# Pair 0 of the first pass: which PSUM bank each of its output blocks is accumulated in

## The chip, the cores and the metric

The kernel runs on one core of a Trainium2 chip. The metric is the device time of that core in microseconds (us). The time before is the median of three runs. One further execution was recorded by the hardware profiler, and every line and duration below comes from it.

The engines are named as in the profile: PE is the matrix engine (TensorE), PEld its weight loads, DVE the vector engine, ACT the scalar engine, POOL the GpSimd engine, SP the engine that issues most of the DMAs. Each takes its own instructions in order and waits for the others by semaphores. PE writes its results to PSUM, and DVE and ACT read them from there.

## The reference, cut to what matters

The input `x` is 128 graphs of 64 nodes with 768 features, and `adj` holds their adjacency matrices. Two layers follow each other. The change is in the first:

```
h   = max(layernorm(x), 0)
ctx = (adj @ (h @ Wadj.T + badj)) / deg + (adj.T @ (h @ Wrev.T + brev)) / rdeg + h @ Wself.T + bself
rel = sum over neighbours of E[adj] @ Wr.T + br * deg  + the same for adj.T with E, Wrr, brr
x   = x + ctx + rel
```

The entries of `adj` are 0 and 1, and the kernel treats them as ids of relations: it counts for each node how many neighbours carry each id and multiplies the counts by a table. The second layer is attention over the graphs with a gate. It is the second pass of the kernel.

## The kernel before, in words

**Tiling.** The 8192 nodes are 64 tiles of 128 rows (two graphs each), and two tiles make a pair. Pass 1 runs over the 32 pairs. The left operand of a pair is cut in six blocks `a00` to `a12`: the first digit is the tile in the pair, the second a third of the 768 inputs. The weights are cut in nine blocks `b00` to `b22` (third of the inputs, third of the outputs). A block product is six fp32 matmuls of 128x128 by 128x256, since a block holds three matrices (`Wadj`, `Wrev`, `Wself`) and two slices of 128 inputs. Each of the six output blocks of a pair (tile, third of the outputs) is then added to `x`.

Pairs 1 to 31 use a scheme with 15 products of sums of blocks (`PRODUCTS`). Pair 0 uses the plain 18 products (`PLAIN`, L73), since the sums of weights (`g10`, `w`, `u`, ...) are only being formed while it runs. Its order is: output block 00, 10, 02, 12, 01, 11, and 18 matmuls for each.

**Banks.** `product` (L741) sends its matmuls to a PSUM bank that has a letter. `new` (L716) makes the tile behind it. Letters a and b each have a tile of their own (`pwa`, `pwb`). Letters c and d are the two halves of one tile, `pwcd`, each half a bank:

```
if not CD:
    CD.append(psw.tile([P, 2, 512], F32, name="pwcd"))
bank[b] = CD[0][:, "cd".index(b)]
```

When an output block is complete, `counts` (L724) adds two bf16 matmuls of relation counts to it, and `add` (L733) has DVE add the bank to `x` (L737). The counts of blocks 00 and 10 are not ready in time in pair 0. They get two steps of their own at the end, `rest_of` (L764), each with a bank, two matmuls (L729) and a DVE add.

**Order.** The order on PE, DVE, ACT and POOL is the order in which the program is written. `main` (L711) gives a list of steps, one matmul each: 0 to 17 are block 00, 18 to 35 block 10, 36 to 53 block 02, 54 to 71 block 12, 72 to 89 block 01, 90 to 107 block 11, and then the two of `rest_of`. `merged` (L248) puts side work between them. For pair 0 that is the list `first` (L884). Of it the following matters here:

- sums of weights on DVE (`weights_sums`) at steps 19, 30, 36, 38, 60, 66 and 76
- `prep_c(1)` at step 40, `count(1, 0)` at 44 and `count(1, 1)` at 52, all DVE work that counts pair 1's ids. `add` of block 02 is at step 53, behind all of these in DVE's order
- `digits(1)` at step 58: four small DVE operations and two POOL copies (`c`, L644)
- `operand` at 54, 64 and 80: pair 1's left operand, by PE (L673) into tiles `pb`, two of which exist, and out of them by ACT (L683)
- `form` at 73 and 91: sums of operand blocks on DVE
- `count_t` at 84 and 92: PE transposes (L652) of the POOL copies

Pair 1 follows at once. Its products begin with banks b, a and d.

Of the kernel before, what the change touches and what calls it, by code (L numbers as in the profile page):

```python
# [69 lines left out]
)  # L70


PLAIN = tuple((f"a{k}{j}", f"b{j}{q}", "abcdab"[2 * i + k], j == 0, f"{k}{q}" if j == 2 else None,  # L73
               "+", i > 0) for i, q in enumerate((0, 2, 1)) for k in range(2) for j in range(3))


# [73 lines left out]
def kernel(  # L150
# [97 lines left out]
    def merged(main, side):  # L248

        side = sorted(side, key=lambda e: e[0])  # L250
        i = 0
        for n, step in enumerate(main):
            while i < len(side) and side[i][0] <= n:
                side[i][1]()
                i += 1
            step()
        for _, step in side[i:]:
            step()
# [135 lines left out]
    with ExitStack() as px:  # L394
# [316 lines left out]
        def main(p):  # L711

            bank = {}
            steps = []

            def new(b):  # L716
                if b in "ab":
                    bank[b] = psw.tile([P, 512], F32, name=f"pw{b}")
                    return
# [4 lines that stand above are left out]
            def counts(b, c, first=False):  # L724
                k, q = int(c[0]), int(c[1])
                if first:
                    new(b)
                for i, (a, e) in enumerate(PARTS):
                    nc.tensor.matmul(bank[b][:, :CQ], CT_T[p, k][: 3 * (e - a), i, :],  # L729
                                     tabs[i][:, q * CQ : (q + 1) * CQ],  # L730
                                     start=(first and i == 0), stop=True, skip_group_check=True)

            def add(b, c, sign="+"):  # L733
                k, q = int(c[0]), int(c[1])
                v = X[2 * p + k][:, q * CQ : (q + 1) * CQ]
                if sign == "+":
                    nc.vector.tensor_add(v, bank[b][:, :CQ], v)  # L737
                else:
                    nc.vector.tensor_sub(v, v, bank[b][:, :CQ])

            def product(an, bn, b, first, c, sign, cnt):  # L741
                def step(q, s):
                    if first and q == s == 0:
                        new(b)
                    nc.tensor.matmul(  # L745
                        bank[b][:, :CQ], OPS[p, an][:, s, q, :],
                        bw[bn][:, (s * KQ + q) * CQ : (s * KQ + q + 1) * CQ],
                        start=(first and q == s == 0), stop=(q == KQ - 1 and s == 2),
                        skip_group_check=True)
                    if q == KQ - 1 and s == 2 and c:  # L750
                        if cnt:
                            counts(b, c)
                        add(b, c, sign)
                for q in range(KQ):
                    for s in range(3):
                        steps.append(lambda q=q, s=s: step(q, s))

            later = (PRODUCTS[1], PRODUCTS[0], *PRODUCTS[2:]) if p + 1 < NP else PRODUCTS  # L760
            for x in later if p else PLAIN:
                product(*x)

            rest_of = ["12"] if p else ["00", "10"]  # L764
            for i, c in enumerate(rest_of):
                b = "dc"[i % 2]
                steps.append(lambda b=b, c=c: (counts(b, c, True), add(b, c)))
            return steps

# [195 lines left out]
        for p in range(NP):  # L965
            merged(main(p), beside(p) if p else first)
# [445 lines left out]
```

## Time and profile before

| | us |
|---|---|
| median of 3 runs | 2400.27 (2399.43 to 2400.63) |
| profiled execution, its own time | 2400.11 |
| its span | 2398.3 |
| PE busy | 2363.1 (99%) |
| DVE busy | 1954.2 (81%) |
| ACT busy | 1339.7 (56%) |
| POOL busy | 380.0 (16%) |

The chain of work that ended last lies on PE for 95% of the span. Times in the trace count from the span's start. Pair 0's products run from 15.05 us to 88.49 us, where the first matmul of pair 1 starts. An fp32 matmul has two records in the trace, so that the six of a block product appear as x12. In lines of the timeline the second number is the time from the first start to the last end of a merged group. Matmuls are pipelined: the next one starts a little before the modelled end of the last.

### The profile page before, as it was taken

The numbers are of one execution on the slowest core, as the hardware profiler recorded it, in microseconds if no ns is written. First come the engines' busy times: TensorE is split into PE (matmuls) and PEld (weight loads), VectorE is DVE, ScalarE is ACT, GpSimd is POOL, SyncE is SP. The second block draws the span as 40 slices with busy tenths as digits, with TensorE's granted clock in tenths as the row PEclk, the third lists the DMA queues.
The fourth block names the chain that finished last, engine by engine and source line by source line (L and its number), as shares of the span: only waits on it lengthen the run. The fifth ranks groups of instructions, "written<-read, shape, count | busy, mean of one in ns | idle before, by whom it ended". The sixth has DMA issues, their size and how long they took to land.

```text
span 2398.3 us, 35465 instructions
## 1 busy us (share of the span) xinstructions
PE 2363.1 (99%) x11777; PEld 1662.7 (69%) x11777; DVE 1954.2 (81%) x3611; ACT 1339.7 (56%) x4017; POOL 380.0 (16%) x983
## 2 busy tenths in 40 slices
PE   7999999999999999999999999999999999999997
PEld 5888888888888888888888884444444444444445
DVE  8677778778778787787787876888989888999999
ACT  2345455454454554544544524777777777767777
POOL 1111111111111111111111111111111111111122
PEclk9999999999999999999999999999999999999999
DMA  5143533534435335344353366665555555555545
GB/s 185 43 121 89 142 99 96 145 89 117 121 89 137 100 95 150 88 109 130 88 136 102 95 189 132 113 113 111 114 110 108 108 111 115 113 110 108 114 98 100
DMA packets 582906, 271.80 MB, mean 113 GB/s; under 512 B 424394, under 2 KB 533053, under 8 KB 582722
## 3 DMA queue, kind: packets, MB, share of 16 engines
q1 hardware_dynamic: 572850, 244.71, 40.3%
q0 software_dynamic: 9728, 24.78, 6.7%
q8 instruction: 93, 1.52, 0.3%
q14 instruction: 91, 0.75, 0.1%
q10 hardware_dynamic: 144, 0.04, 0.0%
HBM read 119.66 MB, written 124.26 MB: 102 GB/s over the span
## 4 chain that ended last, share of the span: by engine, by line
PE 95%; DVE 3%; ACT 2%; issue 0%; DMA 0%; SPq 0%; DVEq 0%; ACTq 0%
PE pwa L745 21%; PE pwb L745 17%; PE pwcd L745 14%; PE pma L1050 13%; PE pmb L1050 11%; PE pmc L1050 5%; PE pmd L1050 4%; PE pb L673 3%; PE ps L1203 2%; PE pwcd L729 1%; PE pwcd L673 1%; PE ps L1185 1%; ACT pr L1102 1%; PE ps L1154 1%; DVE weights L344 0%
## 5 line engine op out<-in xcount | busy, mean ns | idle before, releaser
L745 PE MATMUL pwa<-weights,op 128*128 128x256 f32 x2304 | 539.5, 381 | 0.3 <-DVE x L737 0.3
L745 PEld LDWEIGHTS pwa<-weights,op 128*128 128x128 f32 x2304 | 422.2, 190 | 53.5 <-issue 0.9
L745 PE MATMUL pwb<-weights,op 128*128 128x256 f32 x1932 | 454.2, 381 | 0.0
L745 PEld LDWEIGHTS pwb<-weights,op 128*128 128x128 f32 x1932 | 359.5, 190 | 53.0
L745 PE MATMUL pwcd<-weights,op 128*128 128x256 f32 x1560 | 360.1, 381 | 12.7 <-DVE x L737 12.7
L344 DVE TENSOR_TENSOR op<-op 128x768 f32<-128x768 f32 x310 | 291.8, 950 | 95.6 <-ACT op L683 91.7
L745 PEld LDWEIGHTS pwcd<-weights,op 128*128 128x128 f32 x1560 | 297.6, 191 | 53.9 <-DVE x L737 12.9
L1050 PE MATMUL pma<-weights,op_f 128*128 128x512 f32 x620 | 310.3, 597 | 2.6 <-ACT hh L783 2.2
L683 ACT COPY op<-pb 128x512 f32<-128x512 f32 (+1 forms) x132 | 70.8, 618 | 335.1 <-PE pb L673 335.1
L1102 ACT ACTIVATE pr<-pr 128x128 f32<-128x128 f32 x768 | 225.3, 296 | 25.1 <-DVE pr L1092 25.0
L1050 PEld LDWEIGHTS pma<-weights,op_f 128*128 128x128 f32 x620 | 112.2, 190 | 140.4 <-issue 104.6
L1050 PE MATMUL pmb<-weights,op_f 128*128 128x512 f32 x372 | 193.1, 601 | 0.4 <-DVE hz L1077 0.4
L321 POOL TENSOR_SCALAR rn<-su 128x1 f32<-128x1 f32 x124 | 27.7, 224 | 918.5 <-ACT hf L316 532.1
L531 ACT ACTIVATE hp<-x,rn 128x768 f32<-128x768 f32 x60 | 107.8, 1796 | 108.6 <-POOL rn L323 108.6
L315 ACT ACTIVATE hf<-x 128x768 f32<-128x768 f32 x64 | 53.8, 841 | 164.5 <-DVE x L781 150.2
L1102 ACT ACTIVATION_READ_ACCUMULATOR pr<-pr 128x1 f32 x768 | 144.4, 188 | 0.0
L1175 ACT ACTIVATE pb<-al,mx 128x64 f32<-128x64 f32 x384 | 128.5, 337 | 12.4 <-DVE mx L1167 11.6
L1050 PE MATMUL pmc<-weights,op_f 128*128 128x512 f32 x248 | 129.7, 604 | 0.2 <-DVE weights L1079 0.2
L1213 DVE SCALAR_TENSOR_TENSOR f<-ps,dn,bb 128x128 f32<-128x128 f32 x384 | 110.1, 344 | 21.6 <-PE ps L1203 20.3
L1050 PE MATMUL pmb<-weights,h 128*128 128x512 f32 x248 | 127.7, 596 | 0.0
L737 DVE TENSOR_TENSOR x<-pwa,x 128x256 f32<-128x256 f32 x95 | 40.1, 422 | 104.1 <-PE pwa L729 75.6
L624 DVE TENSOR_REDUCE sum<-eq 128x26 f32<-128x1664 bf16 x64 | 120.0, 1876 | 0.1
(217 smaller groups left out, 3991.1 us busy)
## 6 DMA issues: line engine op xcount, KB each, us to landing
x<-in_x_dram SPq DMA_DIRECT2D x64, 384.0 KB
h<-ht SPq DMA_DIRECT2D x64, 384.0 KB
out_dram<-x SPq DMA_DIRECT2D x64, 384.0 KB
hh<-hh SPq DMA_DIRECT2D x64, 384.0 KB
h<-h SPq DMA_DIRECT2D x256, 96.0 KB
x<-hh SPq DMA_DIRECT2D x64, 384.0 KB
out_dram<-f POOLq DMA_DIRECT2D x62, 384.0 KB, 5.0
h<-hpt SPq DMA_DIRECT2D x60, 384.0 KB
```

Of the source, the lines that this page charges most:

```text
L315: nc.scalar.activation(by, src, AF.Copy, scale=-1.0 / D, accum_out=sums[:, 0:1])
L344: return (nc.vector.tensor_add if s1 == "+" else nc.vector.tensor_sub)(to, x, y)
L531: nc.scalar.activation(hp.rearrange("p (b f i) -> p b f i", b=KB, f=NQ), X[t].rearrange("p (b i f) -> p b f i", b=KB, f=NQ), AF.Relu, scal ...
L624: nc.vector.tensor_reduce(SUM[p][:, k], EQ[p, k], AX.X, OP.add)
L673: nc.tensor.matmul(to[:, g, :, i, :], H0[2 * p + k][o, kb * P : (kb + 1) * P], rts[p % 2][o, k, :n].rearrange("p s n -> p (s n)"), start=T ...
L683: nc.scalar.copy(a[:, :n].rearrange("p s h (g n) -> p g (s h) n", g=GT), ps[:, :, c * n * KQ * N : (c + 1) * n * KQ * N].rearrange("p g (x ...
L745: nc.tensor.matmul(bank[b][:, :CQ], OPS[p, an][:, s, q, :], bw[bn][:, (s * KQ + q) * CQ : (s * KQ + q + 1) * CQ], start=(first and q == s ...
L1050: nc.tensor.matmul(bank[p, b], operand(p, an)[:, q, :], bw2[bn][:, 2 * q * CQ : 2 * (q + 1) * CQ], start=(first and q == 0), stop=(q == KQ ...
L1102: nc.scalar.activation(PR[t][:, j, h, :], PR[t][:, j, h, :], AF.Copy, accum_out=to)
L1175: nc.scalar.activation(PB[t][:, h, :], AL[t][:, h, :], AF.Exp, bias=MX[t][:, h : h + 1], accum_out=DN[t][:, h : h + 1])
L1203: nc.tensor.matmul(po[r][o, c, :], PT[t][s, c, o], (hs if r == g else HX[t])[s, 2 * c + r, :], start=True, stop=True)
L1213: nc.vector.scalar_tensor_tensor(FF[t][:, h * DO : (h + 1) * DO], PO[t][r][:, c, :], DN[t][:, h : h + 1], bb, op0=OP.mult, op1=OP.add)
```

## The change

Only letters change. Pair 0's six output blocks used banks a, b, c, d, a, b and use a, b, c, a, b, c. The two extra count steps used d and c and use a and d. Pairs 1 to 31 keep their letters, `"d" if p else ...` being what `"dc"[0]` was. No instruction is added or removed, and the order on every engine is the same.

```diff
-PLAIN = tuple((f"a{k}{j}", f"b{j}{q}", "abcdab"[2 * i + k], j == 0, f"{k}{q}" if j == 2 else None,
+PLAIN = tuple((f"a{k}{j}", f"b{j}{q}", "abcabc"[2 * i + k], j == 0, f"{k}{q}" if j == 2 else None,
                "+", i > 0) for i, q in enumerate((0, 2, 1)) for k in range(2) for j in range(3))
...
             rest_of = ["12"] if p else ["00", "10"]
             for i, c in enumerate(rest_of):
-                b = "dc"[i % 2]
+                b = "d" if p else "ad"[i]
                 steps.append(lambda b=b, c=c: (counts(b, c, True), add(b, c)))
```

| block or step | bank before | bank after |
|---|---|---|
| 00 | a | a |
| 10 | b | b |
| 02 | c | c |
| 12 | d | a |
| 01 | a | b |
| 11 | b | c |
| counts of 00 | d | a |
| counts of 10 | c | d |

## The prediction

> **What bounds the kernel now.** I read the page first, then the waits of PE, then pair 0 in the timelines of PE and DVE, then the stretches. The page says that PE is the bound, and names one product group with idle time in front of it:
>
> ```profile
> PE 2363.1 (99%) x11777; PEld 1662.7 (69%) x11777; DVE 1954.2 (81%) x3611; ACT 1339.7 (56%) x4017; POOL 380.0 (16%) x983
> ...
> L745 PE MATMUL pwcd<-weights,op 128*128 128x256 f32 x1560 | 360.1, 381 | 12.7 <-DVE x L737 12.7
> ```
>
> Of a span of 2398.3 us PE is idle some 35, and 12.7 of those stand in front of one tile. The waits of PE, longest first, show that this is a single wait, and that the same tile has a small second one:
>
> ```profile
> PE pwcd L745 <- DVE x L737: 12.7, 1, 12.7
> ...
> PE pwcd L729 <- DVE x L737: 0.6, 1, 0.6
> ```
>
> PE's timeline gives the place (start, length, group, idle before it):
>
> ```profile
> 42.75 0.39 PE L729 MATMUL pwcd<-tab,cntT 126*128 126x256 bf16 x2
> 43.07 1.57 PE L673 MATMUL pb<-r,h 64*128 64x192 f32 x16
> 57.29 6.73 PE L745 MATMUL pwcd<-weights,op 128*128 128x256 f32 x20 [12.65 <-DVE x L737]
> 63.95 1.57 PE L673 MATMUL pb<-r,h 64*128 64x192 f32 x16
> 65.45 3.72 PE L745 MATMUL pwcd<-weights,op 128*128 128x256 f32 x16
> ...
> 88.27 0.38 PE L729 MATMUL pwcd<-tab,cntT 126*128 126x256 bf16 x2 [0.62 <-DVE x L737]
> ```
>
> Block 02 (bank c) is complete at 43.1, block 12 (bank d) is next and needs nothing from it. But c and d are one tile, so its first matmul waits until DVE has read block 02. DVE's timeline shows why that is late, and what DVE has to do next:
>
> ```profile
> 55.02 1.89 DVE L624 TENSOR_REDUCE sum<-eq 128x26 f32<-128x1664 bf16 x1
> 56.82 0.41 DVE L737 TENSOR_TENSOR x<-pwcd,x 128x256 f32<-128x256 f32 x1
> ...
> 61.58 1.82 DVE L342 SCALAR_TENSOR_TENSOR weights<-weights 128x1536 f32<-128x1536 f32 x1
> 69.43 0.42 DVE L737 TENSOR_TENSOR x<-pwcd,x 128x256 f32<-128x256 f32 x1 [6.03 <-PE pwcd L729]
> 69.77 2.88 DVE L344 TENSOR_TENSOR op<-op 128x768 f32<-128x768 f32 x3
> 72.57 3.42 DVE L344 TENSOR_TENSOR weights<-weights 128x1536 f32<-128x1536 f32 x2
> 79.29 0.42 DVE L737 TENSOR_TENSOR x<-pwa,x 128x256 f32<-128x256 f32 x1 [3.31 <-PE pwa L729]
> 79.64 2.81 DVE L344 TENSOR_TENSOR op<-op 128x768 f32<-128x768 f32 x3
> 87.46 0.42 DVE L737 TENSOR_TENSOR x<-pwb,x 128x256 f32<-128x256 f32 x1 [5.01 <-PE pwb L729]
> ```
>
> DVE is busy without a break from 41.3 to 63.4 with weight sums and the counting of pair 1. The add stands behind that. Last, the stretches (us; PE, PEld, DVE, ACT, POOL busy; granted clock; DMA share; GB/s):
>
> ```profile
> 44.60:57.30 12.70, 0.05 (x3) 0.01 (x1) 12.32 (x19) 0.93 (x2) 0.00 (x0) 0.63 0.00 0
> 57.30:64.00 6.70, 6.70 (x22) 5.29 (x22) 6.00 (x8) 0.00 (x0) 3.61 (x2) 0.67 0.00 0
> 64.00:69.20 5.20, 5.20 (x35) 4.46 (x35) 0.00 (x0) 1.50 (x2) 0.00 (x0) 1.00 0.00 0
> 88.50:130.00 41.50, 41.50 (x233) 36.09 (x232) 33.17 (x54) 15.12 (x24) 4.54 (x11) 1.00 0.43 118
> ```
>
> The wait has a tail: after it PE runs at a granted clock of 0.67 until 64.0. From 88.5 on PE has no gap for 41.5 us.
>
> **What the Trainium skill says.** "TensorE: Matmul & The Clock Gate", Part 1 (The HAM clock gate): after an idle window of about 3.4 us the array's clock is gated to half, and about 3.4 us of activity release it. The trace agrees in kind: 0.67 for 6.7 us after 12.65 us idle. The same page, under engine queue depths: ACT and DVE are strict FIFO, so the add cannot pass the counting; the trace shows it directly behind. "PSUM — Partial Sum Buffer", Terms: two engines must not touch one bank at once. Here c and d are different banks, so the wait comes from the shared tile and not from that rule; the new letters put PE and DVE on different banks as well.
>
> **The change, part by part.**
>
> *Block 12 goes to bank a.* Bank a was last read by the add of block 00, at 26.99. So nothing holds its first matmul. It starts when the L673 group before it lets it: that group starts at 43.07, and the equal group at 63.95 is followed 1.50 later, so at 44.57 instead of 57.29. That is **12.72** us.
>
> *The slow clock goes too.* The 20 records after the wait take 57.29 to 63.95, 6.66 us. At full clock 12 records take 2.59 (88.49 to 91.08), so 20 take 4.32. That is **2.34** more, and PE is ahead by 15.06 at the L673 group, which now starts at 48.89. The bounds are 0, if the clock is slow there for another reason, and 2.34; I take 2.34, since the stretch before the wait (30 to 44.6) has clock 1.00.
>
> *Is anything late for a PE that is 15.06 ahead?* Operands: ACT has copied out the first `pb` tile by 45.53, before the second group of 48.89; the third group, 72.78 less 15.06 = 57.72, needs a copy that moves with PE to 49.9 to 51.4. DMA: the stretches from 44.6 to 69.2 show a share of 0.00, so the loads have landed. POOL: the two copies that the transposes need run from 58.19 to 61.80, the longer of 1.92, so the first is there by 60.11 and the second by 61.80. They follow DVE, which does not move before 63.4. PE wants them at 76.11 and 79.96 less 15.06, 61.05 and 64.90. It is close, 0.94 us, and costs nothing. Block 01 in bank b waits for the add of block 10 (40.96), block 11 in bank c for that of block 02 (56.82); PE is there at 54.17 and 64.03.
>
> *DVE becomes the late one.* It is free at 63.32 (61.58 + 1.82, less the 0.08 by which neighbours overlap). The add of block 12, which waited for PE until 69.43, finds its bank ready (PE is through at 69.40 less 15.06 = 54.34). Then, with the steps read from the rows above: add 0.34 to 63.66; three operand sums 2.80 to 66.46; two weight sums 3.34 to 69.80; add of block 01 0.34 to 70.14 (PE ready at 64.2); three operand sums 2.73 to 72.87; add of block 11 to 73.29. PE has block 11 ready at 72.36. So DVE arrives half a microsecond behind PE.
>
> *The end of pair 0.* The counts of 00 now go to bank a and start at 87.26 less 15.06 = 72.20. The counts of 10 go to d, in the tile whose half c the add of block 11 is reading: they wait for its end at 73.29 and start 0.06 later (as 88.21 to 88.27 before), at 73.35. This new wait of about 0.8 takes the place of the old 0.62. Queued behind it is all of pair 1 on PE, whose first matmul starts 0.22 later, at 73.57. Before it was 88.49: the sum is **14.92** us. DVE's adds of the two count steps end near 73.6 and 74.2; pair 1's bank a is wanted at 76.2 and bank d at 78.8, so these waits cost nothing.
>
> *Afterwards* pair 1 starts with both engines shifted by about 14.9, and its DMAs (first at 95.20) follow them. No instruction order changes. The gap-free PE carries the shift to the end. The profiled execution would take 2400.11 - 14.92 = 2385.19; the median, 0.16 above it, 2385.35.
>
> **The rivals.**
>
> *The clock's part does not come back, or comes in part.* Then only 12.65 to 13 are gained: 2387.3 to 2387.6. Against it is the 1.00 before the wait.
>
> *DVE or POOL is slower than I copied.* From 41.3 to 73.3 DVE has next to no slack, so each microsecond lost there delays pair 1 by as much; 5% of the 32 us is 1.6, giving 2387.0. A late POOL copy costs only what goes beyond 0.94. For it speaks that the POOL copies took 1.9 us here and 0.39 elsewhere, so neighbours disturb each other; against it that DVE's companions up to 63.4 are the same.
>
> *The change does nothing or is eaten later.* Were bank a held by something, or did pair 1 wait for a DMA at a fixed time, the time would be 2398 to 2400. The only DMA-bound starts I find follow the engines that move.
>
> *Slower.* One mechanism: PE now works from 15 us on without the 12.65 us pause, and the granted clock falls under the load. PE is busy some 2363 us, so the gain is gone when the mean granted clock goes from 0.996 to 0.990, and below 0.988 the time is over 2405. Against it are 2300 us at 99% busy with a clock of 1.00.
>
> **How the numbers follow.** Chances: the sum as worked out 0.80 (own range 2384.3 to 2386.3), the clock's part lost 0.06, DVE or POOL later 0.08, nothing 0.03, slower 0.03. Below the sum lies the case that DVE is not behind at all, 15.06 + 0.62 = 15.7, 2384.6; with the runs' spread of about 0.8 the low end is 2383.7. The high end takes in the first two rivals with that spread, 2388.2. Within 0.2% (4.8 us) is about what a measurement cannot tell from no change; faster by more is 0.94, within 0.03, slower 0.03.
>
> **What would show it.** Right: no PE wait over 1 us before 130; the L745 group after 43.07 starts near 44.6 with tile `pwa` and 20 records in 4.3; clock 1.00 from 44.6; DVE without idle time from 63.4 to 73; one PE wait of 0.5 to 1 before the last L729 group near 73.3; the first L745 of pair 1 near 73.6. Wrong: a wait at the L652 transposes near 61 (POOL), or one at block 12 on something else. If pair 1 starts near 73.6 and the span is not shorter by the same, the gain was eaten later.

## The result, and the profile after

| | before | after |
|---|---|---|
| median, us | 2400.45 (4 runs) | 2385.38 (4 runs) |
| second comparison, us | 2400.74 (9 runs) | 2385.34 (5 runs) |
| profiled execution: span, us | 2398.3 | 2383.3 |

The ratio is 0.994 with a 95% interval of 0.9922 to 0.9957, and 0.9938 (0.9926 to 0.9951) in the second comparison. The changed kernel is some 15 us faster; the prediction was 2385.35. That the median lies within 0.03 of it is chance: its four runs lie between 2385.01 and 2387.75.

The page of the changed kernel, in the rows that answer to those of before:

```profile
PE 2359.6 (99%) x11777; PEld 1660.7 (70%) x11777; DVE 1954.0 (82%) x3611; ACT 1339.6 (56%) x4017; POOL 381.6 (16%) x983
...
L745 PE MATMUL pwcd<-weights,op 128*128 128x256 f32 x1560 | 357.8, 379 | 0.0
```

The idle time in front of the `pwcd` products is 0.0 in place of 12.7. PE is also 3.5 us less busy with the same 11777 records, of which some 2.1 are the slow clock after the wait; the runs don't show what the rest is. Of PE's waits in pair 0 on this tile only the small one is left:

```profile
PE pwcd L729 <- DVE x L737: 0.5, 1, 0.5
```

PE's timeline of the changed kernel, around block 12 and at the end of pair 0 (start, length, group, idle before it):

```profile
42.42 1.57 PE L673 MATMUL pb<-r,h 64*128 64x192 f32 x16
43.92 4.58 PE L745 MATMUL pwa<-weights,op 128*128 128x256 f32 x20
48.44 1.57 PE L673 MATMUL pb<-r,h 64*128 64x192 f32 x16
...
71.52 0.39 PE L729 MATMUL pwcd<-tab,cntT 126*128 126x256 bf16 x2
71.74 0.38 PE L729 MATMUL pwa<-tab,cntT 126*128 126x256 bf16 x2
72.67 0.38 PE L729 MATMUL pwcd<-tab,cntT 126*128 126x256 bf16 x2 [0.55 <-DVE x L737]
72.89 2.75 PE L745 MATMUL pwb<-weights,op 128*128 128x256 f32 x12
```

Block 12 now follows the L673 group at once, and its 20 records take 4.52 us up to the next group, not 6.66. The rest of the order is as before. The last group is the first product of pair 1. DVE's timeline of the same stretch:

```profile
60.94 1.82 DVE L342 SCALAR_TENSOR_TENSOR weights<-weights 128x1536 f32<-128x1536 f32 x1
62.68 0.41 DVE L737 TENSOR_TENSOR x<-pwa,x 128x256 f32<-128x256 f32 x1
63.02 2.87 DVE L344 TENSOR_TENSOR op<-op 128x768 f32<-128x768 f32 x3
65.81 3.42 DVE L344 TENSOR_TENSOR weights<-weights 128x1536 f32<-128x1536 f32 x2
69.14 0.41 DVE L737 TENSOR_TENSOR x<-pwb,x 128x256 f32<-128x256 f32 x1
69.48 2.81 DVE L344 TENSOR_TENSOR op<-op 128x768 f32<-128x768 f32 x3
72.20 0.42 DVE L737 TENSOR_TENSOR x<-pwcd,x 128x256 f32<-128x256 f32 x1
```

No row has idle time in front of it: DVE, which before was idle 6.03, 3.31 and 5.01 us ahead of the adds of blocks 12, 01 and 11, works through and is just behind PE at 72.20. In the stretches, the clock (the number after the busy times) is 1.00 where it was 0.63 and 0.67:

```profile
44.60:57.30 12.70, 12.70 (x71) 10.51 (x69) 12.29 (x23) 1.79 (x3) 0.00 (x0) 1.00 0.00 0
57.30:64.00 6.70, 6.70 (x43) 5.76 (x43) 6.62 (x6) 1.93 (x4) 3.61 (x2) 1.00 0.01 2
```

**A ruler for what follows.** The start of the span is not the same to a microsecond in every execution: the L673 group at the head of the wait starts at 43.07 before, at 42.42 after. So I measure from the start of that group to the start of pair 1's first product, and call it the stretch. It is 88.49 - 43.07 = 45.42 before and 72.89 - 42.42 = 30.47 after: 14.95 less. The spans differ by 15.0: 14.95, plus 0.65 for the earlier start, less 0.60 because the part behind the stretch took 2309.81 us before and 2310.41 after.

### The profile page after: what moved, and what is told of

It reads as the page before. It is cut to its first block, busy times and chain, and to the rows that moved or that the text cites. A ratio compares the mean times of both kernels' runs of the same rounds, so it can differ in the third digit from the quotient of the medians.

```text
span 2383.3 us, 35466 instructions
## 1 busy us (share of the span) xinstructions
PE 2359.6 (99%) x11777; PEld 1660.7 (70%) x11777; DVE 1954.0 (82%) x3611; ACT 1339.6 (56%) x4017; POOL 381.6 (16%) x983
## 4 chain that ended last, share of the span: by engine, by line
PE 93%; DVE 3%; ACT 1%; DMA 1%; issue 0%; SPq 0%; POOL 0%; DVEq 0%; POOLq 0%; ACTq 0%
PE pwa L745 20%; PE pwb L745 17%; PE pwcd L745 13%; PE pma L1050 13%; PE pmb L1050 11%; PE pmc L1050 5%; PE pmd L1050 4%; PE pb L673 2%; PE ps L1203 2%; PE pwcd L729 1%; PE pwcd L673 1%; PE ps L1185 1%; ACT pr L1102 1%; PE ps L1154 1%; DVE weights L344 1%
```

## The experiments

The theory: block 12 waits because its bank shares a tile with the bank of block 02, and the read of block 02 stands behind a long queue on DVE; the idle time then also gates PE's clock; with both gone, DVE sets the end of pair 0 by a small margin. The rivals: bank d itself, or the sharing of the tile whatever DVE does; another cause for the slow matmuls; a gain that needs both edits.

**The whole change again.**

> The changed kernel once more, beside the kernel before. Theory (shared tile behind a long DVE queue, plus the slow clock after the idle time): 15.0 us less than before, ratio 0.9938. Rival (part of the difference is chance of the runs): under 13 us.

The ratio, 0.9938, is given above. By time alone the rival isn't excluded, since the interval leaves room for 11.8 to 17.8 us. The stretch does exclude it: it is 73.30 - 42.82 = 30.48, 14.94 less than before, and the part behind it took 2309.8, as in the kernel before. So the 0.60 above belongs to that execution and not to the change.

**One half at a time.** The letters of the six blocks alone:

```diff
-PLAIN = tuple((f"a{k}{j}", f"b{j}{q}", "abcdab"[2 * i + k], j == 0, f"{k}{q}" if j == 2 else None,
+PLAIN = tuple((f"a{k}{j}", f"b{j}{q}", "abcabc"[2 * i + k], j == 0, f"{k}{q}" if j == 2 else None,
...
                 b = "dc"[i % 2]
```

> Only the letters of the six output blocks change (a, b, c, a, b, c); the two count steps keep d and c. Theory: block 12 no longer waits, but at the end the counts in d wait for the add of block 11 from c, and the counts in c for the add from d. Pair 1 starts some 0.9 us later than in the changed kernel, at about 73.8 in its span: 14.2 us less than before, some 2386.2. Rival (the gain needs both edits, since the tile is still in use twice at the end): most of the 12.7 us wait turns up at the end of pair 0.

Measured: 2387.41 (2386.39 to 2388.14), ratio 0.9946 (0.993 to 0.9961). In PE's timeline the two count steps of this kernel each wait for an add:

```profile
73.06 0.38 PE L729 MATMUL pwcd<-tab,cntT 126*128 126x256 bf16 x2 [0.77 <-DVE x L737]
73.96 0.38 PE L729 MATMUL pwcd<-tab,cntT 126*128 126x256 bf16 x2 [0.52 <-DVE x L737]
```

The stretch is 74.18 - 42.81 = 31.37, 0.89 longer than with both edits, as expected. The times agree in direction; their ranges overlap, so the size is read from the trace.

The letters of the count steps alone:

```diff
 PLAIN = tuple((f"a{k}{j}", f"b{j}{q}", "abcdab"[2 * i + k], j == 0, f"{k}{q}" if j == 2 else None,
...
-                b = "dc"[i % 2]
+                b = "d" if p else "ad"[i]
```

> Only the letters of the two count steps change (a and d for d and c); block 12 stays in d. Theory: the wait of 12.65 us and the slow clock stay, the last wait of 0.62 us goes: 0.6 us less than before, within what a run can tell. Rival (the sharing at the end matters more than it looks): several us less.

Measured: 2400.23 beside 2400.46, ratio 0.9999 (0.9991 to 1.0008): no difference. The last wait is gone, and the stretch is still 87.57 - 42.17 = 45.40. The end gained 0.56, but this execution lost as much to the slow clock: the 20 records after the wait took 7.20 us (56.39 to 63.59), not 6.66. So the gain of the change lies in the block letters, and the other edit is worth 0.9 us only once they are changed.

**Bank d or the shared tile.** The changed kernel with block 12 in d as before, and block 02 in a:

```diff
-PLAIN = tuple((f"a{k}{j}", f"b{j}{q}", "abcabc"[2 * i + k], j == 0, f"{k}{q}" if j == 2 else None,
+PLAIN = tuple((f"a{k}{j}", f"b{j}{q}", "abadbc"[2 * i + k], j == 0, f"{k}{q}" if j == 2 else None,
```

> The changed kernel with the blocks in a, b, a, d, b, c: block 12 is in bank d as before, but block 02 is in a. Theory (what costs is the other half of the tile being unread, not bank d): no wait at block 12, pair 1 starts as in the changed kernel, near 72.9 to 73.6, and the time is 2385.4. Rival (bank d): a wait of some 12 us, 2400.

One run: 2384.69. Block 12 runs in `pwcd` with no wait:

```profile
42.25 1.57 PE L673 MATMUL pb<-r,h 64*128 64x192 f32 x16
43.75 4.58 PE L745 MATMUL pwcd<-weights,op 128*128 128x256 f32 x20
```

The stretch is 72.73 - 42.25 = 30.48. Bank d is not the cause; what costs is that bank c, the other half of its tile, is unread. No run gave c and d a tile each. That the common tile ties the two banks, and not something else about this pair, is read from the program and not shown.

**The DVE queue.** The letters of before, with the counting of pair 1 behind the add of block 02:

```diff
-(44, lambda: count(1, 0)),
+(54, lambda: count(1, 0)),
...
-(52, lambda: count(1, 1)),
+(54, lambda: count(1, 1)),
```

> The letters of the kernel before; the counting of pair 1's ids on DVE is written after the add of block 02 and no longer ahead of it. Theory: the shared tile alone costs little, the DVE queue ahead of the add makes the wait. PE waits some 2.3 us for the add (from 44.6 to 46.9), the clock stays at 1.00, and pair 1 starts near 75.8: 12.7 us less than before, 2387.7. Rival (bank d or the shared tile itself is slow, whatever DVE does): the wait stays near 12.7 us and the time near 2400.

Measured: 2391.93 (2391.8 to 2392.64), ratio 0.9964 (0.995 to 0.9978). The rival falls, but my numbers missed too. PE's timeline of this kernel:

```profile
43.12 1.57 PE L673 MATMUL pb<-r,h 64*128 64x192 f32 x16
49.26 6.27 PE L745 MATMUL pwcd<-weights,op 128*128 128x256 f32 x20 [4.57 <-DVE x L737]
55.47 1.57 PE L673 MATMUL pb<-r,h 64*128 64x192 f32 x16
```

The wait is 4.57, not 2.3: I had overlooked `prep_c(1)` at step 40, nine small DVE operations that also stand ahead of the add and take 2.3 us. And the 20 records took 6.21 us (clock 0.73 from 49.2 to 55.5), 1.69 more than in the changed kernel. The stretch is 36.88, 8.54 less than before. To see whether these two explain the miss, `prep_c(1)` was moved as well:

```diff
-(40, lambda: prep_c(1)),
+(54, lambda: prep_c(1)),
```

> The letters of the kernel before; the preparation of pair 1's ids (2.3 us on DVE) now stands behind the add of block 02 as well, as all of the counting did in the run with the add first. Theory (that run missed its number because PE still waited 4.57 us, which was long enough for the clock to be gated, at 1.9 us more): PE waits some 2.3 us, the clock stays at 1.00, the 20 records take 4.5 us, and pair 1 starts 12.5 us sooner after its L673 group at 43: 12.5 us less than before, 2388. Rival (the slow 20 records of that run have another cause, so that a short wait does not spare them): 20 records in over 6 us, 10.4 us less than before, 2390.

Measured: 2388.85 (2387.44 to 2389.08) beside 2399.83, ratio 0.9954 (0.9938 to 0.9971). By time alone 12.5 and 10.4 can't be told apart, but PE's timeline does it:

```profile
42.67 1.57 PE L673 MATMUL pb<-r,h 64*128 64x192 f32 x16
46.50 4.58 PE L745 MATMUL pwcd<-weights,op 128*128 128x256 f32 x20 [2.26 <-DVE x L737]
51.01 1.57 PE L673 MATMUL pb<-r,h 64*128 64x192 f32 x16
```

Behind this wait of 2.26 the next 20 records run at full speed. The stretch is 75.55 - 42.67 = 32.88, 12.54 less than before. So the same tile with the same sharing costs little once DVE comes to the add early: the queue ahead of the add makes the wait. The clock was lost behind the wait of 4.57 and kept behind that of 2.26, in one execution each.

**The clock alone.** The kernel before, with PE kept at work in the idle time by 28 fp32 matmuls into bank a whose results nothing uses:

```diff
+if p == 0 and (an, bn, q, s) == ("a10", "b02", 0, 0):
+    new("a")
+    for _ in range(28):
+        nc.tensor.matmul(bank["a"][:, :CQ], OPS[p, an][:, 0, 0, :], bw[bn][:, :CQ],
+                         start=True, stop=True, skip_group_check=True)
```

> The kernel before, with 28 more fp32 matmuls of 128x128 by 128x256 into bank a ahead of block 12, whose results are not used; they fill 12.1 of the 12.65 us in which PE waits. Theory (the 20 records after the wait are slow because the clock was gated in the idle time): the stretch has clock 1.00, the 20 records take 4.3 us in place of 6.66, 2.3 us less than before, 2398.1. Rival (they are slow because DVE and POOL work beside them): 6.66 us as before, no difference.

Measured: 2398.69 (13 runs) beside 2400.46 (25 runs), ratio 0.9993 (0.9985 to 1.0001). PE's timeline of this kernel, the filler first:

```profile
44.70 12.35 PE L746 MATMUL pwa<-weights,op 128*128 128x256 f32 x56
57.42 4.58 PE L750 MATMUL pwcd<-weights,op 128*128 128x256 f32 x20 [0.37 <-DVE x L737]
61.94 1.57 PE L673 MATMUL pb<-r,h 64*128 64x192 f32 x16
```

The product starts as late as before, with DVE and POOL at the same work beside it, and its 20 records take 4.52 us. The stretch is 86.47 - 43.20 = 43.27, 2.15 less than before. The time points the same way by 1.8, with an interval that just reaches no difference. In the trace the clock, 1.00 from 44.7 to 61.9, is thus the cause of the slow matmuls, and its part of the gain is 2.1 us.

**Which engine is late at the end of pair 0.** The changed kernel with 3.34 us of weight sums moved off DVE's pair 0:

```diff
-(76, lambda: weights_sums("g11", "g3")),
...
-more += [(8, lambda: weights_sums("g9")), (25, lambda: weights_sums("g1"))]
+more += [(8, lambda: weights_sums("g3", "g9")), (25, lambda: weights_sums("g1")),
+         (30, lambda: weights_sums("g11"))]
```

> The changed kernel with two weight sums (g11 and g3, 3.34 us of DVE) moved from pair 0 into pair 1. Theory (at the end of pair 0 DVE is later than PE by some 0.3 to 0.9 us): the PE wait before the last counts falls from 0.55 to about 0.3 us, and pair 1 starts about 0.25 us sooner after the first L673 group of pair 1 at 42 to 43. Rival (PE was the later one): the wait is unchanged.

One run: 2385.99. In PE's timeline the last wait is shorter, and DVE is now the one that waits for block 11:

```profile
72.74 0.38 PE L729 MATMUL pwcd<-tab,cntT 126*128 126x256 bf16 x2 [0.29 <-DVE x L737]
...
72.27 0.42 DVE L737 TENSOR_TENSOR x<-pwcd,x 128x256 f32<-128x256 f32 x1 [2.99 <-PE pwcd L729]
```

The stretch is 72.96 - 42.74 = 30.22, 0.26 less than 30.48. So DVE was the later engine by about a quarter of a microsecond. The whole time doesn't show it.

**The last wait taken out.** The changed kernel with both count steps ahead of block 11, in the two halves of bank a (in `main`, for pair 0; `counts` gets an argument `start`, which lets its first matmul start a new sum):

```diff
...
+def early(old=steps[90]):
+    new("a")
+    for i, c in enumerate(rest_of):
+        bank[i] = bank["a"][:, i * CQ : (i + 1) * CQ]
+        counts(i, c, start=True)
+    old()
+steps[90] = early
+steps += [lambda i=i, c=c: add(i, c) for i, c in enumerate(rest_of)]
...
```

> The changed kernel with the two count steps moved ahead of block 11, both into bank a, one in each half; their adds stay at the end. Theory: the last PE wait of pair 0 (0.55 us in the changed kernel) is gone and pair 1 starts 0.7 us sooner; 0.7 us less than the changed kernel, 2384.7, which is hardly to be told from the runs' spread. Rival (DVE, which is behind PE there, makes pair 1 wait as much later): no difference.

Measured: 2385.14 (2384.59 to 2386.8), ratio 0.9936 (0.9924 to 0.9949), beside 2385.34 for the changed kernel in the same comparison. In the trace the stretch is 72.92 - 43.15 = 29.77, 0.71 shorter, as expected. In time it can't be told from the changed kernel.

## Why the prediction was right

**Block 12 in bank a, 12.72.** As predicted: it starts 1.50 after the L673 group, and nothing else holds it.

**The slow clock, 2.34.** The mechanism is shown by the filler; the size was 2.14. I took the full-speed time of the 20 records, 4.32, from a steady run of products, but they need 4.52 (4.51 in some) in every kernel with a full clock. The 0.2 lies at the ends: the first record takes 0.32 us to the next one and the last 0.31 to the L673 group behind it, all others 0.22. I had also read the 0.67 as a clock that held until 64.0. It is a mean: the clock was 0.50 until 61.7 and 1.00 after. The sum used only the 6.66 and is not touched by this.

**Nothing late for PE.** Right. The first POOL copy took at most 1.92 from 57.55, so was there by 59.47, and PE came at 60.60, with no wait.

**DVE becomes the late one.** Right in kind, and its own chain was right to 0.02: the add of block 11 starts 29.78 after the L673 group, where the sum said 72.87 - 43.07 = 29.80. PE was 0.2 later than thought (the clock term), so the new wait was 0.55, not 0.8. That is why the two misses cancel: where DVE sets the end, what PE does sooner or later by 0.2 doesn't matter. The sum was 14.92, the stretch gave 14.95. The margin is thin, though. The run with less DVE work shows DVE only 0.26 behind, so a PE later by more than that would have moved the end, and an agreement to 0.03 is better than the terms were.

**Afterwards.** The shift carries through: pair 31's first product starts at 1400.60 before and 1385.02 after, 1312.11 and 1312.13 behind pair 1's.

**The rivals.** The lost clock and the disturbed DVE didn't occur. Nor did a lower granted clock under the load: its mean rose from 0.996 to 0.998, which fits the stretch at 0.50 that is gone.

## What to carry to other kernels

A wait of PE is worth more than its length where the clock is lost behind it, and less where another engine comes into the lead. Follow that engine's queue row by row from the point where it stops waiting; here that sum held to a tenth of a microsecond. Two banks in one tile were one buffer to the waits of this program, and the price of that depended on what stood ahead of the read in the reader's queue. Letters, or the order on the reader, both cure it, here for 15.0 and 12.5 us in the traces (15.1 and 11.0 by the medians, the latter with room for 7 to 15). Count everything ahead of the read, small operations too.

## What the runs showed of the hardware that I had not expected

- What the slow clock cost did not follow from the length of the wait: 1.69 us after 4.57, and 2.14 and 2.68 after the same 12.65 in two executions. It is about half of the time for which the clock stayed at 0.50 once PE was back at work: 3.4, 4.4 and 5.5 us. After the wait of 4.57 the clock fell only when PE had been back for 0.3 us, at 49.6 (stretches of the kernel with the counting alone behind the add; the clock is the number after the busy times):

```profile
44.70:49.20 4.50, 0.00 (x0) 0.00 (x0) 4.33 (x13) 0.89 (x2) 0.00 (x0) 1.00 0.00 0
49.20:49.50 0.30, 0.24 (x1) 0.24 (x2) 0.30 (x2) 0.00 (x0) 0.00 (x0) 1.00 0.00 0
49.60:52.90 3.30, 3.30 (x9) 2.64 (x8) 3.23 (x3) 0.00 (x0) 0.00 (x0) 0.50 0.00 0
53.00:55.50 2.50, 2.50 (x14) 1.94 (x12) 2.40 (x4) 0.00 (x0) 0.00 (x0) 1.00 0.00 0
```

- Nor does the length alone decide whether the clock is lost. At the start of the second pass PE waits 2.2 us for ACT in all eleven profiled executions. In nine the clock stayed at 1.00 there. In two, the letters of the count steps alone and the filler, it fell to 0.50 for 3.4 us as PE came back, which cost 1.7 us. Both lines are from the former:

```profile
1447.68 2.04 PE L1050 MATMUL pma<-weights,op_f 128*128 128x512 f32 x2 [2.24 <-ACT hh L783]
...
1447.70:1451.00 3.30, 3.30 (x4) 1.46 (x5) 1.84 (x4) 2.23 (x5) 0.20 (x2) 0.50 1.21 168
```

- The part of the kernel behind pair 0 took 2309.8 to 2310.8 us in nine of the eleven profiled executions and 2312.0 in these two, though its order is the same in ten of them (in the kernel with less DVE work two sums moved into pair 1). Differences of under 1 us in pair 0 are therefore to be read in the trace, from a mark near by.
